# First layer of a four-layer hybrid kernel: tents and masks made in the fourth slot, an image's statistics drawn apart over slots, wide tokens of the last image in half the slots

## The chip, the cores and the metric

The kernel runs on one core of one Trainium2 chip. The metric is the device time of one execution in microseconds; the time given for a kernel is the median of several runs. Beside the times there is one profiled execution, with a record of every instruction on the five engines: PE (TensorE matmul, with PEld for its weight loads), DVE (VectorE), ACT (ScalarE), POOL (GpSimd) and SP (SyncE, which here issues transfers).

## The reference

The input `x` is 4 images of 128 channels by 64 x 64 pixels, float32. Four layers follow each other; the change is in layer 0 alone, so only that one is told in full.

```python
# layer 0: x = x + dcn(group_norm(x))
val = xf @ w_value + b_value                      # 128 channels per token
om  = xf @ w_off + b_off                          # per group (8): 9 offsets (x, y), 9 masks
sy, sx = base_y + offset_y, base_x + offset_x     # 3x3 taps, moved by the offsets
acc = sum over 4 corners: gather(val, corner) * bilinear_weight * inside
out = (acc * mask).sum(over 9 taps) @ w_out + b_out
out = batch_norm(out);  return out * sigmoid(out)
# layer 1: 1x1 conv, depthwise conv, two-way Mamba scan, batch norm, gate
# layers 2 and 3: a token attention and a mixture of experts, each with layer norms
```

Layer 0 is a deformable convolution: each token reads nine places around it, each shifted by an offset that is computed from the token itself.

## The kernel before

Layer 0 works without gathers for nearly all tokens. A token whose offsets stay within one pixel reads only from a 5 x 5 neighbourhood, so its output is a sum of 25 shifted copies of the value map, each times a weight per token and group. The weights come from tent functions of the offsets. The few tokens with larger offsets ("wide tokens") are gathered apart, image by image, and added in.

**Rounds and slots.** Each image is cut into 8 quads of 4 row pairs (`TG` = 4), so there are 32 rounds, `r` = 0 to 31, with four warm-up rounds before and one closing round behind. A round has five slots, `k` = 0 to 4. The order of the instructions on each engine is the order in which the loop writes them: the helper class `InOrder` passes each operation on with a request to keep it in program order, and for that reason all records of layer 0 carry line L85, the helper's own, and are told apart by their tiles. An engine thus stands at an instruction until its inputs are there, and everything behind it on that engine stands too.

What one round does, by engine:

- DVE: five products `pr`, one a slot (`multiply(r, k+1)` in slots 0 to 2, and in the last slot `multiply(r+1, 0)`), each 128 x 2560; in slot 0 `flags(a)` of the round before (it reduces the offsets `omw` to `wide`, compares into `fl`, and counts in `cum`), and after it the generator `weights`, which multiplies the tents by the masks (`tent<-tent,masks`), and over slots 0 to 2 makes `Q` and the weights `wt` of round r+1.
- PE: `accumulate(r, k)`, 20 transposing matmuls a slot that sum the products into `acc`; `project(a, k)`, the projection of the quad `a` = r + 8 (an image ahead) to values and offsets; and small matmuls for ranks and wide tokens.
- ACT: in slot 2 the copy `near_w` of `wt` into PSUM, which the next round's products read; `evict(a, k-1)` in slot k, two copies `omw` and `vb` out of PSUM each, the fourth in slot 4; `onehot` (`ohc`, `ohs`); `finish` (`sl`, a Silu) and `aT`; in slot 3 the copy `xr` (`order`); and at the end of slot 4 `tents(...)` and `near(...)`, the tents `tent`, `ab` and the masks `masks` of round r+2 (four instructions of 128 x 576 for the tents and four small ones for the masks).
- POOL: five pieces of the products (`piece<-v,wt`), the addition of finished quads to `X`, and the indirect gathers of the wide tokens.
- SP: all loads of shifted value tiles `v`, the stores and loads of the offsets.

Buffers bound what can run ahead: `pr` and the gathered `px` have two each, `tent`, `masks` and `wt` have one.

**Side work, one step a slot.** Three generators are advanced by one step in each slot: `weights`; `statistics(n)`, which computes the group-norm statistics of image n and folds them into its weights (`bn_stats` over the image, a matmul `pg` to sum over a group, a second `pg2`, the root `rstd` on ACT, a matmul `pb`, then `bs`, `bn`, `wn` on DVE); and `exceptions(n)`, the wide tokens of an image, which starts in the image's second round: two gathers, tents, weights, then seven times a multiplication of `px` on DVE, seven transposes on PE and the next gather. For image 2 the statistics start in round 3, for image 3 in round 11. All eight `bn_stats` are written in one slot.

**Finishing.** A quad can be finished (`onehot`, then `spread`, `finish`, `settle` in the following slots) when its image's wide tokens are done; the table `ends` says in which round. `flags` and `evict` run for rounds 0 to 23 only, because the last image has nothing ahead of it.

**The end.** `reached` computes from `wide` and `cum` whether any token had larger offsets than the method covers (`m`, `pst`, `pm`, `mm`, `over`); it is written in slot 1 of round 31. The generator `maps_steps`, small work on DVE and PE that prepares matrices for later layers (`omw`, `plm`, `vb`, `xr` as scratch), starts in round 32, two steps a slot. Layer 1 starts behind it.

Of the kernel before, what the change touches and what calls it, by code (L numbers as in the profile page):

```python
# [8 lines left out]
F32 = mybir.dt.float32  # L9
# [8 lines left out]
P = 128  # L18
NB = 4
# [75 lines left out]
class Kernel:  # L95
# [33 lines left out]
    def layer0(self):  # L129
# [8 lines left out]
        R, R2 = 1, 2  # L138
# [11 lines left out]
        with ExitStack() as outer:  # L150
            fp = outer.enter_context(tc.tile_pool(name="d0x", bufs=1))
            over = fp.tile([1, 1], I32, name="over")
            with ExitStack() as ctx:
# [115 lines left out]
                def statistics(n, nc):  # L269

                    xn = X[:, n * L:(n + 1) * L]
                    st = sm.tile([P, 8, 6], F32, name="st", bufs=1)
                    for c in range(8):
                        nc.vector.bn_stats(st[:, c, :], xn[:, c * 512:(c + 1) * 512])
                    mv = sm.tile([P, 2], F32, name="mv", bufs=1)
                    nc.vector.bn_aggr(mv, st)
                    yield
                    pg = pp.tile([P, 512], F32, name="pg", tag="pp")
                    nc.tensor.matmul(pg[:, 0:2], gm, mv, start=True, stop=True)
                    gmv2 = sm.tile([P, 2], F32, name="gmv2", bufs=1)  # L280
                    nc.vector.tensor_copy(gmv2, pg[:, 0:2])
                    d = sm.tile([P, 1], F32, name="d", bufs=1)
                    nc.vector.tensor_sub(d, mv[:, 0:1], gmv2[:, 0:1])
                    nc.vector.tensor_mul(d, d, d)
                    yield
                    pg2 = pp.tile([P, 512], F32, name="pg2", tag="pp")
                    nc.tensor.matmul(pg2[:, 0:1], gm, d, start=True, stop=True)
                    rstd = sm.tile([P, 1], F32, name="rstd", bufs=1)
                    nc.vector.tensor_add(rstd, gmv2[:, 1:2], pg2[:, 0:1])
                    nc.scalar.activation(rstd, rstd, AF.Sqrt, bias=self.eps5)  # L290
                    yield
                    nc.vector.reciprocal(rstd, rstd)
                    ms = sm.tile([P, P], F32, name="ms", bufs=1)
                    nc.vector.tensor_scalar(ms, self.ones, gmv2[:, 0:1], rstd, ALU.mult, ALU.mult)
                    yield
                    pb = pp.tile([P, 512], F32, name="pb", tag="pp")
                    nc.tensor.matmul(pb[:, 0:NWO], ms, w, start=True, stop=True)


                    bs = wp.tile([P, 2, NWO], F32, name="bs", tag="t0")  # L300
                    nc.vector.tensor_sub(bs[:, 0], brow, pb[:, 0:NWO])
                    nc.vector.tensor_copy(bs[:, 1].bitcast(F32R), bs[:, 0])
                    nc.vector.tensor_sub(bs[:, 0], bs[:, 0], bs[:, 1])
                    nc.vector.tensor_scalar(bs[:, 1], bs[:, 1], self.ident[:, 0:1], None, ALU.mult)
                    bn = cp.tile([P, NWO], F32R, name="bn", bufs=2)
                    nc.vector.scalar_tensor_tensor(bn, bs[:, 0], self.ident[:, 1:2], bs[:, 1], ALU.mult, ALU.add)
                    wn = cp.tile([P, NWO], F32, name="wn", bufs=2)
                    nc.vector.tensor_scalar(wn, w, rstd, None, ALU.mult)
                    maps[n] = (wn, bn)
# [336 lines left out]
                ends = {}  # L646
                for i in range(NB * NQS):
                    n, q = divmod(i, NQS)
                    k = 5 + q if n < NB - 1 else (5, 5, 6, 6, 7, 7, 7, 8)[q]
                    ends.setdefault(n * NQS + k, []).append(i)  # L650
                extra, stat, tent, wgen, mask = None, None, None, None, None
                held = marked = None
# [2 lines left out]
                for r in range(-4, LAST_R + 1):  # L655
# [6 lines left out]
                        extra = exceptions(r // NQS)  # L662
                    if r == -3:
                        stat = statistics(1, nc)
                    if r >= 0 and r % NQS == 3 and r // NQS + 2 < NB:
                        stat = statistics(r // NQS + 2, nc)
                    live = 0 <= r < LAST_R
                    coming = 0 <= r + 1 < LAST_R
# [12 lines left out]
                        later_maps = self.maps_begin(left_over)  # L681
                    if 1 <= r <= LAST_R:
                        turn(r - 1)
                    if r == LAST_R:
                        later_maps = self.maps_steps(
                            nc, later_maps, lambda: pp.tile([P, 512], F32, name="plm", tag="pp"))

                    for k in range(W):
                        if live:
                            for u in PIECES.get(k, ()):  # L690
                                accumulate_piece(r)
                            if k < W - 1:
                                accumulate(r, k)
                            if k < W - 2:
                                multiply(r, k + 1)
                        if k == 0 and r > 0:
                            for a in before if before and before[0] >= NQS else ():
                                flags(a)
                        if coming and k < 3:
                            next(wgen)  # L700
                            if k == 2:
                                nc.scalar.copy(near_w, wts[r + 1][:, 1:W - 1])
                        if r <= 0 and before:
                            for a in before if k == 0 else ():
                                rank(a)
                            if k in (1, 3):
                                early = onehot(*which(before[k // 2]), "ohc")
                            if k in (2, 4):
                                collect(before[k // 2 - 1], early)
                        if r < 0 and k < TG:  # L710
                            a = ahead[k // 2]
                            if k % 2 == 0 and a not in ordered:
                                order(a)
                            for h in (0, 1):
                                project(a, 2 * (k % 2) + h)
                            for h in (0, 1):
                                evict(a, 2 * (k % 2) + h)
                        for a in ahead if r >= 0 else ():
                            if k:
                                evict(a, k - 1)  # L720
                            if k < TG:
                                if k == 0 and a not in ordered:
                                    order(a)
                                project(a, k)
                        if stat is not None:
                            next(stat, None)
                        if r > 0:
                            if k == 1:
                                for a in before:
                                    rank(a)  # L730
                            if k == 2:
                                ohc = [onehot(*which(a), "ohc") for a in before]
                            if k == W - 1:
                                for a, oh in zip(before, ohc):
                                    collect(a, oh)
                        if r > 0:
                            if held is not None:
                                settle(held[0], finish(*held))
                                held = None
                            if marked is not None:  # L740
                                i, oh = marked
                                held, marked = (i, spread(i, oh)), None
                            if fins:
                                i = fins.pop(0)
                                marked = i, onehot(*divmod(i, NQS), "ohs", 2)
                            if r == LAST_R - 1 and k == W - 2:
                                fins = ends.pop(LAST_R)
                        if k == TG - 1 and nxt is not None and nxt < NB * NQS:
                            order(nxt)
                        if k == W - 1:  # L750
                            if 0 <= r + 2 < LAST_R and r >= -1:
                                tent, mask = tents(read[r + 2], M, R), near(r + 2)
                            if coming:
                                multiply(r + 1, 0)
                            for a in ahead if r < 0 else ():
                                flags(a)
                        if extra is not None:
                            next(extra, None)
                        if r == LAST_R - 1 and k == 1:
                            reached(nc)  # L760
                        if r == LAST_R:
                            for _ in range(2):
                                next(later_maps, None)
                    before = ahead
# [2068 lines left out]
```

## Time and the profile before

| | |
|---|---|
| time, median of 3 runs | 4961.55 us (4955.89 to 4970.51) |
| the profiled execution's own time | 4962.14 us |
| its span | 4960.0 us |
| mean granted TensorE clock | 0.947 |
| layer 0 in the span | 0 to 860 us; layer 1's first work at 865.5 |
| a steady round (round 8) | 284.14 to 305.42, 21.28 us |
| round 3, round 11 (statistics of images 2 and 3) | 38.85 us, 40.03 us |
| rounds 26 to 28 together | 63.75 us |
| busy in the span | PE 4500.3 us, DVE 3590.7, ACT 3614.6, POOL 3039.9 |

A round is counted from the start of its first product (`pr<-v,wt` on DVE) to the next one. The busy times are of the whole span, so they say little of layer 0, which is a sixth of it. A record has the start in us, the length in us, engine, line, operation, the tile written and the tiles read, the shape and how many alike; in brackets stands how long the engine was idle before it and what released it.

### The profile page before, as it was taken

The page shows a single profiled execution, that of the slowest core. Times are in us where ns is not written, and L with a number is a line of the kernel's source. Part 1 is how long each engine was busy: PE and PEld are TensorE (multiplying, and loading weights), DVE is VectorE, ACT ScalarE, POOL GpSimd, SP SyncE. Part 2 cuts the span into 40 slices and gives each one's busy share as a digit, 9 for nine tenths or more (in the row PEclk, how much of TensorE's full clock was granted, in tenths as well). Part 3 has the DMA queues.
Part 4 walks back from the last instruction along what each step waited for, and adds up shares of the span by engine and source line. Part 5 has one row for each costly group of instructions (what it writes and reads, how often), then busy time and mean ns, then how long its engine had stood idle before and what let it go on. Part 6 is the DMA issues. An engine that isn't in the chain of part 4 may idle for free. (4 is left out here: it accounts for less than half of the span.)

```text
span 4960.0 us, 66029 instructions
## 1 busy us (share of the span) xinstructions
PE 4500.3 (91%) x22570; PEld 2441.0 (49%) x22570; DVE 3590.7 (72%) x7202; ACT 3614.6 (73%) x5503; POOL 3039.9 (61%) x3047
## 2 busy tenths in 40 slices
PE   6788887798899699998897999999999999999798
PEld 4677765465566344443343444444444444444344
DVE  5998996689877578884775666666666666665675
ACT  4455553455555577776675999999999999999575
POOL 1232333155556345553587888888888888878488
PEclk9999999879779799999899999999999999999899
DMA  6666773000000300000000000000000000000000
GB/s 210 165 181 164 184 190 102 5 1 18 11 7 18 96 12 0 1 1 1 18 18 34 1 1 1 1 1 1 1 1 1 1 1 1 1 1 1 7 28 35
DMA packets 65940, 188.39 MB, mean 38 GB/s; under 512 B 12020, under 2 KB 15284, under 8 KB 63924
## 3 DMA queue, kind: packets, MB, share of 16 engines
q1 hardware_dynamic: 60020, 167.89, 12.0%
q0 software_dynamic: 2240, 12.85, 0.9%
q8 instruction: 182, 2.98, 0.3%
q10 hardware_dynamic: 3328, 3.28, 0.2%
q14 instruction: 170, 1.39, 0.1%
HBM read 133.23 MB, written 50.74 MB: 37 GB/s over the span
## 5 line engine op out<-in xcount | busy, mean ns | idle before, releaser
L85 POOL TENSOR_TENSOR r<-r 128x512 f32<-128x512 f32 (+1 forms) x1088 | 1349.2, 1242 | 331.5 <-DVE r L85 267.9
L85 DVE TENSOR_TENSOR r<-r,num 128x1024 f32<-128x1024 f32 (+1 forms) x1088 | 975.2, 927 | 599.6 <-PE num L85 507.5
L85 PE MATMUL D<-F,G 32*128 32x512 f32 (+3 forms) x4608 | 1138.8, 573 | 1.8 <-DVE den L85 0.9
L85 PE MATMUL num<-F,G 32*128 32x512 f32 (+3 forms) x4608 | 1057.2, 590 | 6.8 <-DVE r L85 3.9
L85 ACT ACTIVATE r<-r 128x2048 f32<-128x2048 f32 (+4 forms) x610 | 1018.5, 1679 | 50.9 <-POOL r L85 4.3
L85 ACT ACTIVATE r<-D 128x1536 f32<-128x1536 f32 (+1 forms) x544 | 763.3, 1403 | 50.2 <-PE D L85 29.8
L85 PEld LDWEIGHTS D<-F,G 32*128 32x128 f32 x4608 | 484.5, 184 | 372.9 <-issue 233.7
L85 PE MATMUL acc<-r,v 128*128 128x512 f32 (+3 forms) x1152 | 598.1, 606 | 0.7 <-ACT r L85 0.7
L85 POOL TENSOR_TENSOR x<-x 128x512 f32<-128x512 f32 (+2 forms) x320 | 405.4, 1267 | 146.7 <-DVE m L85 65.0
L85 PEld LDWEIGHTS num<-F,G 32*128 32x128 f32 x4608 | 383.4, 183 | 222.4 <-issue 110.8
L85 PE MATMUL pff<-hid,w_ffn_w2T 128*128 128x512 f32 x1024 | 469.4, 601 | 0.0
L85 PE MATMUL pex<-w_expert_w,vT 128*128 128x512 f32 x1024 | 460.8, 598 | 1.6 <-DVE x L85 1.4
L85 POOL TENSOR_TENSOR piece<-v,wt 128x512 f32<-128x512 f32 x160 | 167.6, 1066 | 380.3 <-DVE cum L85 90.5
L85 PEld LDWEIGHTS acc<-r,v 128*128 128x128 f32 x1152 | 174.1, 188 | 382.7 <-issue 186.7
L85 PE MATMUL acc<-ident,pr 128*128 128x128 f32 x2560 | 320.7, 283 | 42.3 <-DVE pr L85 42.3
L85 ACT ACTIVATE x<-pex,gate 128x128 f32<-128x128 f32 x896 | 256.7, 367 | 101.2 <-PE pex L85 75.7
L85 PEld LDWEIGHTS acc<-ident,pr 128*128 128x128 f32 x2560 | 299.4, 146 | 54.2 <-DVE pr L85 51.7
L85 ACT ACTIVATE hid<-phh,cols 128x512 f32<-128x512 f32 x416 | 252.8, 688 | 68.2 <-PE phh L85 68.0
L85 PEld LDWEIGHTS pex<-w_expert_w,vT 128*128 128x128 f32 x1024 | 190.6, 192 | 216.6 <-issue 160.6
L85 PEld LDWEIGHTS pff<-hid,w_ffn_w2T 128*128 128x128 f32 x1024 | 185.3, 191 | 201.6 <-issue 201.6
L85 DVE TENSOR_TENSOR pr<-v,near_w 128x2560 f32<-128x2560 f32 x96 | 269.9, 2812 | 0.1
L85 POOL TENSOR_TENSOR Y<-y,tm 128x64 f32<-128x64 f32 x256 | 113.3, 463 | 232.2 <-DVE y L85 125.7
(482 smaller groups left out, 7906.6 us busy)
## 6 DMA issues: line engine op xcount, KB each, us to landing
v<-tab SPq DMA_DIRECT2D x320, 256.0 KB
oms<-omw SPq DMA_DIRECT2D x32, 432.0 KB
omr<-oms SPq DMA_DIRECT2D x32, 432.0 KB
X<-in_x_dram SPq DMA_DIRECT2D x8, 1024.0 KB
tab<-vb SPq DMA_DIRECT2D x64, 128.0 KB
o<-o SPq DMA_DIRECT2D x32, 256.0 KB
oin<-o SPq DMA_DIRECT2D x32, 256.0 KB
kept<-X SPq DMA_DIRECT2D x4, 2048.0 KB
```

The lines of the kernel that those rows point to most:

```text
L85: self.last = op(*args, **kwargs)
```

## The change

It has four edits, all in the order of layer 0's instructions; no arithmetic is added or taken away.

1. Tents and masks of round r+2 are written in slot 3 (`W - 2`), ahead of that slot's `evict`, and not at the end of slot 4. In the rounds with r % 8 = 1 in which wide tokens are on, they are written in slot 4, but ahead of its `evict`.
2. The statistics of images 2 and 3 start a round earlier (r % 8 = 2), with two `bn_stats` a slot, and with one more slot after each of the three small matmuls.
3. From round 26 on, the wide tokens go forward by two steps a slot. The last image's quads are finished a round or so earlier (the table `ends`).
4. `reached` moves from slot 1 of round 31 to slot 3, and `maps_steps` starts there, two steps a slot.

```diff
 # statistics(n)
                     for c in range(8):
                         nc.vector.bn_stats(st[:, c, :], xn[:, c * 512:(c + 1) * 512])
+                        if n > 1 and c % 2:
+                            yield
...
                     nc.tensor.matmul(pg[:, 0:2], gm, mv, start=True, stop=True)
+                    if n > 1:
+                        yield
...
                     nc.tensor.matmul(pg2[:, 0:1], gm, d, start=True, stop=True)
+                    if n > 1:
+                        yield
...
                     nc.tensor.matmul(pb[:, 0:NWO], ms, w, start=True, stop=True)
+                    if n > 1:
+                        yield
...
 # the loop over rounds
-                    k = 5 + q if n < NB - 1 else (5, 5, 6, 6, 7, 7, 7, 8)[q]
+                    k = 5 + q if n < NB - 1 else (4, 4, 5, 5, 6, 6, 7, 8)[q]
...
-                    if r >= 0 and r % NQS == 3 and r // NQS + 2 < NB:
+                    if r >= 0 and r % NQS == 2 and r // NQS + 2 < NB:
                         stat = statistics(r // NQS + 2, nc)
...
-                    if r == LAST_R:
-                        later_maps = self.maps_steps(
-                            nc, later_maps, lambda: pp.tile([P, 512], F32, name="plm", tag="pp"))
...
+                        if k == (W - 2 if extra is None or r % NQS != 1 else W - 1) and 0 <= r + 2 < LAST_R and r >= -1:
+                            tent, mask = tents(read[r + 2], M, R), near(r + 2)
                         for a in ahead if r >= 0 else ():
                             if k:
                                 evict(a, k - 1)
...
                         if k == W - 1:
-                            if 0 <= r + 2 < LAST_R and r >= -1:
-                                tent, mask = tents(read[r + 2], M, R), near(r + 2)
                             if coming:
                                 multiply(r + 1, 0)
...
-                        if extra is not None:
-                            next(extra, None)
-                        if r == LAST_R - 1 and k == 1:
+                        for _ in range(1 if r < LAST_R - NQS + 2 else 2):
+                            if extra is not None:
+                                next(extra, None)
+                        if r == LAST_R - 1 and k == W - 2:
                             reached(nc)
-                        if r == LAST_R:
+                            later_maps = self.maps_steps(
+                                nc, later_maps, lambda: pp.tile([P, 512], F32, name="plm", tag="pp"))
+                        if r == LAST_R - 1 and k >= W - 2 or r == LAST_R:
                             for _ in range(2):
                                 next(later_maps, None)
```

## The prediction

> **What bounds the kernel now.** I read the busy table by windows of the first layer first (the change touches nothing behind it: on every engine the instruction order after layer 0 is the same). Layer 0 ends at 860 of the 4960.0 us.
>
> ```profile
> core 0: us, PE busy (x) PEld busy (x) DVE busy (x) ACT busy (x) POOL busy (x), PEclk, DMA share, GB/s
> 240.00:290.00 50.00, 44.69 (x303) 37.98 (x302) 45.37 (x41) 33.23 (x90) 15.18 (x15) 0.97 0.67 175
> ```
>
> DVE is busy 45.4 of 50 us and ACT 33.2. PE shows 44.7, but its own waits are for DVE's products. So a microsecond of DVE idle time is a microsecond of the layer, and the next view is what DVE waits for between 110 and 870 us (total, times, longest).
>
> ```profile
> DVE tent L85 <- ACT masks L85: 26.1, 18, 3.0
> DVE omw L85 <- POOL omw L85: 11.9, 1, 11.9
> DVE bs L85 <- PE pb L85: 11.1, 2, 5.6
> DVE rstd L85 <- PE pg L85: 3.4, 2, 1.8
> DVE m L85 <- PE pst L85: 3.2, 1, 3.2
> DVE rstd L85 <- ACT rstd L85: 1.3, 2, 0.9
> DVE wide L85 <- ACT omw L85: 0.5, 1, 0.5
> ```
>
> These are what the change aims at: the masks, the statistics (`bs`, `rstd`) and the end of the layer (`omw`, `m`). The last line is the one to keep in mind: once, `flags` had to wait for `evict`. Third view, one undisturbed round (8) on ACT, then on DVE:
>
> ```profile
> 284.05 0.56 ACT L85 COPY near_w<-wt 128x480 f32<-128x480 f32 x1 [1.88 <-DVE wt L85]
> 288.43 0.35 ACT L85 COPY omw<-psp 128x216 f32<-128x216 f32 x1
> 288.94 0.81 ACT L85 ACTIVATE tent<-omr,shift 128x576 f32<-128x576 f32 x1
> 291.79 1.08 ACT L85 ACTIVATE masks<-omr,fine 128x72 f32<-128x72 f32 x4
> 292.77 0.57 ACT L85 COPY aT<-acc 128x512 f32<-128x512 f32 x1
> ```
>
> ```profile
> 289.62 0.75 DVE L85 TENSOR_REDUCE wide<-omw 128x4 f32<-128x576 f32 x1
> 290.40 0.66 DVE L85 TENSOR_SCALAR fl<-wide 128x4 f32<-128x4 f32 x1
> 292.90 1.06 DVE L85 TENSOR_TENSOR tent<-tent,masks 128x864 f32<-128x864 f32 x1 [1.39 <-ACT masks L85]
> ```
>
> From `near_w` at 284.05 to the masks' end at 292.87 ACT never pauses; it is a chain of 8.8 us that starts when DVE ends `wt`. DVE has only two products (2.8 us each) and `flags` to put beside it, and idles 1.39 us. `wide` reads the fourth `evict` copy (288.43 to 288.79), and had 0.83 us to spare.
>
> **Part 1, tents and masks ahead of `evict(a, 2)`.** Nothing is added or removed; on ACT tents and masks (292.77 − 288.94 = 3.83 us) go ahead of the last two `evict`s, so these move back by 3.83. The fourth copy ends at 288.79 + 3.83 = 292.62. In DVE's order `flags` stands before the multiplication by the masks, and still reads that copy: the queue behind it is that multiplication, then `Q`, then the next product. `wide` starts at 292.65 instead of 289.62, takes 0.75, and with `fl` and two `cum` 1.31 us (so measured at 143.44 to 144.75, where POOL ran no piece). The masks' multiplication starts at 293.96, where before it started at 292.90: +1.06 us a round. The wait on masks goes, but one on `evict` that is longer takes its place. If `fl` still ran 0.66 us (it ran while POOL multiplied two pieces, 288.94 to 291.03), it would be +1.6.
>
> It holds in the rounds that have an `evict` and no other slack: 1, 5 to 9, 13 to 17, 21 to 24, 15 rounds, +16. Rounds 2, 4, 10, 12, 18 have 6 to 8 us between copy and `wide`, and pay nothing; 3 and 11 lie behind the statistics; from 25 on nothing is evicted and the masks' wait (mostly under 0.5 there) goes for nothing. In round 13 the chain takes in one more table load for Silu (1.28 us at 384.34, which stood in round 11), in rounds 19 and 20 some 0.6 us. Sum +17.7; bounds +13 (`flags` finds slack in a few rounds) and +26 (`fl` stays slow).
>
> The Trainium skill, SBUF — State Buffer, Terms, calls the read and write port pair of DVE and GpSimd an exclusive lock held for a whole instruction; the 0.66 us of `fl` beside a POOL piece (0.17 elsewhere) agrees, and as the pieces would then run in DVE's idle time the rule speaks for 1.06.
>
> **Part 2, statistics.** The same eight `bn_stats`, spread over four slots of rounds 2 and 10, and four more slots between the short steps. Before, in round 3:
>
> ```profile
> 187.50 0.16 DVE L85 TENSOR_TENSOR rstd<-gmv,pg 128x1 f32<-128x1 f32 x1 [1.76 <-PE pg L85]
> 188.02 0.16 DVE L85 RECIPROCAL rstd<-rstd 128x1 f32<-128x1 f32 x1 [0.36 <-ACT rstd L85]
> 195.21 0.51 DVE L85 TENSOR_TENSOR bs<-brow,pb 128x344 f32<-128x344 f32 x1 [5.64 <-PE pb L85]
> ```
>
> The two rounds idle 15.8 us in these waits. The `pb` wait goes, as `bs` comes a slot later. But the square root is now in ACT's queue behind `near_w` (0.5), an `evict`, the tents (3.83) and another `evict`, and the reciprocal, in the last slot, waits: counted from the end of `wt` at 185.74, the next `pr` started 12.18 later before; now the reciprocal at about +7.4, the `pr` at +7.9, and 2.7 us of `bs`, `bn`, `wn` still to come in round 4. Gain 1.55. In round 11 the same with `sl` 0.67 and the table load 1.28 ahead of the root: 12.49 before, 12.58 after, loss 0.1. Sum −1.5; bounds −15.8 (every wait hidden) and +3 (one more table change of 1.28 a time).
>
> **Part 3, wide tokens of the last image, two steps a slot from round 26.** Seven multiplications of 1.08 us, 49 transposes and five gathers, the same number; only closer together.
>
> ```profile
> px<-tab,idx POOLq DMA_INDIRECT x28, 6.8
> ```
>
> A gather lands 6.8 us after its issue (median; single ones 4.4 to 11.2). There are two `px` buffers, so tile s+2 needs the multiplication of s (1.1), its transposes behind PE's queue (about 2.5) and the gather: 10.4 us. Two slots last 8.5 us (rounds 26 to 28 took 63.75 us, 15 slots). So DVE stalls some 2 us at every second one of the five later tiles, three times: +6. Until now a tile had four slots, 17 us. Bounds +0.5 (landing in 4.4) and +10 (landing in 11.2, with the products queued behind on DVE).
>
> The Trainium skill, DMA: Bandwidth & Descriptors, "Anatomy of one DMA — SWDGE (gpsimd) path", gives 2.0 us plus bytes over 436e3: by it a gather of 459 KB takes an estimated 3.05 us, nothing would stall, and the sum below would be some 6 us less; the trace's 6.8 is what I use.
>
> **Part 4, the end.** The images' last `finish` steps come one round earlier (three in round 28). PE then stands behind `oT`, which ACT copies after the tents: some 1.5 us in round 29 and 0.2 in 30, while masks' waits of about 1.5 go: +0.2, bounds −1 and +4. At the end of the layer:
>
> ```profile
> 829.52 0.22 DVE L85 COPY omw<-ident 128x128 f32<-128x128 f32 x1
> 841.67 0.40 DVE L85 TENSOR_SCALAR omw<-omw 128x1 int32<-128x1 int32 x5 [11.94 <-POOL omw L85]
> ```
>
> The small chain of layer 1's maps starts at 841.67 and ends at 859.94; it takes 18.3 us, and layer 1 starts behind it. Without `reached` (822.05 to 826.84) ahead of it the last product ends 4 us sooner, about 824.9; the last sum on PE ends at 832.8, `reached` at 834.5, and the chain starts at about 834.8, its steps two a slot from round 31. −6.9; bounds −4 (the chain meets the last sums on PE) and −11 (its small matmuls, which ran at half clock: granted 0.64 in 850 to 870, weight loads 0.34 us where others take 0.19, run at full).
>
> **Sum.** 17.7 − 1.5 + 6 + 0.2 − 6.9 = +15.5. The profiled execution took 4962.14 us (0.6 above the median of three, 4961.55, which ran from 4955.89 to 4970.51); the forecast is 4961.55 + 15.5 = 4977. No change that a measurement can tell is ±0.3%, 4946.7 to 4976.4, so the forecast sits on its upper edge.
>
> **Rivals.**
> 1. Faster: `flags` doesn't gate. Place: DVE's `wide` in slot 0. Price: then the 26.1 us on masks go whole, −26.1 − 1.5 + 6 + 0.2 − 6.9 = −28, 4933. It decides at the fourth copy's end: up to 289.62 in round 8's time `wide` waits for nothing. For: the masks' wait is real, 18 times. Against: the copy is put at 292.62 by adding ACT's own rows, with no pause among them to absorb it, and round 6 shows the wait already (0.5). Chance 0.08.
> 2. No difference: `flags` costs its 13 to 17, but the statistics' waits go by half (−8), gathers land early (+1) and the end gains 9: 0, with a range of ±8, about 4962. For: 15.8 us of visible waits, and half clock at the end. Against: ACT's queue ahead of the root. 0.20.
> 3. Much slower: the `fl` collision stays (+8.5), and the gathers land late (+10 instead of +6) with PE's in-order queue behind the transposes (+4): 4992 to 5000. For: gathers of 11.2 us are in the trace. Against: they are few. 0.17.
>
> My own case has 0.55, 4967 to 4987, half of it above the bound: 0.29 slower and 0.26 the same. With rival 2 wholly within (0.17; 0.01 faster, 0.02 slower) and rival 3 slower: slower 0.48, same 0.43, faster 0.09. Range: from 4954, which takes in most of rival 2, to 4995, which takes in the low end of rival 3.
>
> **What would show it.** Right: DVE's `wide` waiting for ACT's `omw` some 15 times, about 3 us each; the masks' wait near zero; a steady round of 22.35 us where it was 21.28; `rstd` waiting for ACT's `rstd` twice, several us; `px` waiting for its gather in rounds 26 and 27; the maps' chain starting about 7 us sooner against the last product. Wrong: a steady round shorter than 21.28 (rival 1); statistics rounds of 3 and 11 shorter by 5 us or more (rival 2); DVE idle by over 4 us at one `px` (rival 3).

## The result, and the profile after

The changed kernel takes 4989.04 us (median of 8 runs, 4983.89 to 4996.12); the kernel before, run beside it, 4961.09 us (8 runs). The ratio is 1.0058, 95% interval 1.0045 to 1.0071: slower by 28 us (22 to 35). The forecast was 4977, slower by 15.5; 4989 lies inside the forecast's range (4954 to 4995) and just above the 4967 to 4987 of its own case.

First the waits of DVE in the changed kernel, from 110 us to the end of layer 0 (total, times, longest):

```profile
DVE wide L85 <- ACT omw L85: 47.4, 17, 4.6
DVE rstd L85 <- ACT rstd L85: 13.5, 2, 9.0
DVE pr L85 <- PE acc L85: 9.9, 8, 2.6
DVE px L85 <- DMA px<-tab,idx: 6.8, 2, 5.7
DVE m L85 <- PE pst L85: 4.9, 1, 4.9
DVE tent L85 <- ACT masks L85: 3.2, 2, 1.8
```

The three largest waits that the change aimed at are gone or small: masks 26.1 to 3.2, `bs` on `pb` 11.1 to nothing, `omw` on POOL 11.9 to nothing. (`rstd` still waits for `pg`, 3.5 us, and `m` waits longer than before.) In the place of each stands a new one. Round 8 on ACT shows the first:

```profile
287.74 0.56 ACT L85 COPY near_w<-wt 128x480 f32<-128x480 f32 x1 [1.88 <-DVE wt L85]
291.23 0.76 ACT L85 ACTIVATE tent<-omr,shift 128x576 f32<-128x576 f32 x1
294.04 1.08 ACT L85 ACTIVATE masks<-omr,fine 128x72 f32<-128x72 f32 x4
295.92 0.34 ACT L85 COPY omw<-psp 128x216 f32<-128x216 f32 x1
```

and the same round on DVE:

```profile
296.29 0.75 DVE L85 TENSOR_REDUCE wide<-omw 128x4 f32<-128x576 f32 x1 [2.89 <-ACT omw L85]
297.07 0.17 DVE L85 TENSOR_SCALAR fl<-wide 128x4 f32<-128x4 f32 x1
297.61 1.05 DVE L85 TENSOR_TENSOR tent<-tent,masks 128x864 f32<-128x864 f32 x1
```

The masks are done at 295.1, but the multiplication that reads them starts at 297.61: `flags` stands ahead of it in DVE's order and waits 2.89 us for the fourth `evict`, which is now the last of ACT's chain. `fl` takes 0.17 us, not 0.66. The round lasts 22.29 us, 1.01 more than before.

By stages of layer 0, from the rounds' starts in the two profiled executions (us):

| stage | before | after | difference | forecast |
|---|---|---|---|---|
| rounds 0, 1, 5 to 9, 13 to 25 | 458.5 | 474.9 | +16.4 | +17.7 |
| rounds 2 to 4 (statistics) | 81.9 | 80.5 | -1.4 | -1.55 |
| rounds 10 to 12 (statistics) | 83.1 | 86.1 | +3.0 | +0.1 |
| rounds 26 to 28 (wide tokens) | 63.8 | 76.7 | +12.9 | +6 |
| rounds 29 and 30 | 39.4 | 44.2 | +4.8 | +0.2 |
| round 31 to layer 1 | 51.6 | 44.7 | -6.9 | -6.9 |
| together | 778.3 | 807.1 | +28.8 | +15.5 |

Layer 1 is counted here from its first instruction on POOL (at 865.48 us in the kernel before). In runs below that change nothing in rounds 2 to 4 and 10 to 12, these two stages take 80.4 to 81.9 and 83.1 to 85.6 us, so up to 1.5 and 2.5 us of their differences can be variation between executions.

### The profile page after: what moved, and what is told of

It reads as the page before. It is cut to its first block, busy times and chain, and to the rows that moved or that the text cites. A ratio compares the mean times of both kernels' runs of the same rounds, so it can differ in the third digit from the quotient of the medians.

```text
span 4986.8 us, 66012 instructions
## 1 busy us (share of the span) xinstructions
PE 4504.9 (90%) x22570; PEld 2445.7 (49%) x22570; DVE 3589.0 (72%) x7202; ACT 3616.0 (73%) x5503; POOL 3041.8 (61%) x3047
```

## The experiments

Each time is given against the kernel before, run beside it on the same chip (there its median was 4954 to 4956 us). Stage times are from one profiled execution each. Some stretches vary between executions of the same instructions: the warm-up ahead of round 0 by up to 4 us, the two statistics stages by up to 2.5, round 31 to layer 1 by up to 6 (47.8 to 53.8 us where nothing was changed there), and all that stands behind layer 0 by up to 24 (4077 to 4101 us). So stages are compared from round to round, and whole times by the ratios alone.

**1. Each edit by itself.** Four kernels, the kernel before with one of the four edits of the diff above.

> Only edit 1: tents and masks ahead of the fourth slot's evict; all else as before. Theory (flags wait for the evict that now stands behind the tents): DVE's wide waits for ACT's omw some 3 us in each of the 15 rounds with an evict and without slack, a steady round is 22.3 us, and the statistics rounds 3 and 11, in which pb waits for a PSUM buffer that an evict frees, become up to 3.8 us longer each. Together +18 to +26 us. Rival (the moved statistics bring most of the wait on wide with them, the tents alone cost little): +10 or less, a steady round of 21.3 us or shorter.

Measured 1.0032 (1.0020 to 1.0043), +16 us. From round 0 to the start of round 31 it lost 17.85 us; a steady round lasts 22.30 us, and `wide` waits 49.2 us in 19 places. Of the 17.85, 15.2 lie in the rounds of the table's first line. The theory holds, the rival falls. Of the extra loss in the statistics rounds there is less than I allowed: +0.4 in round 3, +2.4 in round 11, where either round varies by up to 1.5 between executions.

> Only edit 2: statistics a round earlier and spread over slots; tents stay at the end of slot 4. Theory (the root stood in ACT's queue behind the tents, which cost 3.83 us in round 3 and as much in round 11): without the tents ahead of it rounds 2 to 4 together are 5 us shorter than before and rounds 10 to 12 about 1 us shorter; -6 us in all. Rival (the wait for the root is made by the other work ahead of it in the queue, Silu's wait for PE and a table load): about +1.6 us as in the whole change, -1.4 and +3.0.

Measured 0.9990 (0.9978 to 1.0003), which doesn't tell it from no change. The root is reached earlier without the tents, as the theory says: its wait is 0.71 us in round 3 and 5.27 in round 11, where the changed kernel has 4.49 and 9.05. But the rounds do not get shorter by that: rounds 2 to 4 gain 2.0 us, rounds 10 to 13 lose 1.8, and most of both can be variation between executions. Part of it came back at once, in round 4:

```profile
196.40 2.60 DVE L85 TENSOR_TENSOR_SCAN cum<-ones,cum,fl 128x4 f32<-128x4 f32 x1
196.90 2.07 POOL L85 TENSOR_TENSOR piece<-v,wt 128x512 f32<-128x512 f32 x2
```

The first line is DVE's, the second POOL's. `cum` is 0.23 us elsewhere; here it ends with POOL's two pieces, which themselves stood behind a gather. So the theory named the queue rightly, and its -6 us are not there.

> Only edit 3: the last image's wide tokens two steps a slot from round 26, and its quads finished a round earlier. Theory (gathers that land too late for the two px buffers, and POOL pieces that start late behind a gather and then hold up DVE): rounds 26 to 28 some 13 us longer than before and rounds 29 and 30 some 5 us longer, as in the whole change; +17 us. Rival (rounds 29 and 30 lost because tents stand ahead of the finishing in ACT's queue): +13 us and rounds 29 and 30 as before.

Measured 1.0026 (1.0012 to 1.0041), +13 us. Rounds 26 to 28 are 14.8 us longer, rounds 29 and 30 5.5. The rival falls: tents stand in slot 4 here, and rounds 29 and 30 lose as much. What I had not expected is behind them: round 31 to layer 1 is 13.5 us shorter, without the fourth edit.

> Only edit 4: reached and the maps' small chain from slot 3 of round 31. Theory: the last product ends 4 us earlier and the chain starts behind the last sum instead of after the closing round's other work; layer 1 starts 7 us earlier, -7 us. Rival (the layer's end is set by the sums and the finishing of the last quads, not by the chain): within 2 us of before.

Measured 1.0004 (0.9994 to 1.0014): no gain. The maps' chain does start sooner, 24.2 us after the start of round 31 where the kernel before and the run with the statistics alone have 27.8. But it then takes 18.7 us, where those two have 17.9 and 15.1. The end of the layer is 3.3 us shorter in its profile, but 3.8 in that of the statistics alone, where nothing at the end was changed, so no gain at the end can be put down to the edit. The theory's 7 us are refuted; by the interval the edit alone gains at most 3.

**2. Is it flags?**

```diff
-                        if k == 0 and r > 0:
-                            for a in before if before and before[0] >= NQS else ():
-                                flags(a)
                         if coming and k < 3:
                             next(wgen)
                             if k == 2:
                                 nc.scalar.copy(near_w, wts[r + 1][:, 1:W - 1])
+                        if k == 0 and r > 0:
+                            for a in before if before and before[0] >= NQS else ():
+                                flags(a)
```

> The changed kernel with flags(a) written behind the first step of weights (masks and Q) instead of ahead of it. Theory (the changed kernel's rounds are held by flags, which wait for the evict behind the tents, with the masks' multiplication queued behind them): the wait of wide on omw falls from 2.9 us to under 0.5, the multiplication waits for the masks instead, which end at about 7.4 us after near_w, some 1.9 us; a steady round of about 21.1 us, 1.2 us less than the changed kernel, -17 us against it, that is +8 to +12 us against the kernel before. Rival (evict itself is late for other users, PE's PSUM buffers or the store of the offsets): steady round stays at 22.3 us.

Measured 1.0037 (1.0023 to 1.0050), +18 us where the changed kernel has +28. Round 8 on DVE:

```profile
290.95 1.06 DVE L85 TENSOR_TENSOR tent<-tent,masks 128x864 f32<-128x864 f32 x1 [1.75 <-ACT masks L85]
293.69 0.75 DVE L85 TENSOR_REDUCE wide<-omw 128x4 f32<-128x576 f32 x1
```

`wide` waits for nothing, the multiplication for the masks, 1.75 us; the round is 21.20 us (expected 21.1). For the round that is the theory, nearly to its numbers; `flags` was what held it. The gain on the changed kernel is less than the theory's 17 us: some 10 by the two ratios, 11.7 by the profiles from round 0 to the start of round 26. The run also says why the place in slot 3 could never bring much: from `near_w` to the masks' end ACT still needs 7.4 us, and DVE has two products, 5.6 us, to put beside it. In the kernel before, `flags` filled that gap.

**3. Another place for the tents.** Two kernels, the kernel before with one edit each: tents and masks in slot 1 behind the second step of `weights`, and at the head of slot 2 (in both, rounds with r % 8 = 1 keep them in slot 4, since the wide tokens use the same buffers then). The code below is the second's; its comment says how the first differs.

```diff
+                        if k == 2 and 0 <= r < LAST_R - 2 and r % NQS != 1:    # or: k == 1, behind next(wgen)
+                            tent, mask = tents(read[r + 2], M, R), near(r + 2)
                         if coming and k < 3:
                             next(wgen)
```

> The kernel before with one edit: tents and masks written in slot 1, behind the second step of weights, where ACT is idle for 6 us of a round (in rounds with r % 8 = 1 at the end of slot 4 as before). Theory (what matters is the length of ACT's chain from near_w to whatever DVE needs first; the tents fit into ACT's idle time before near_w): the wait on masks goes without a new one on omw, a steady round of 19.9 to 20.3 us, -18 to -26 us. Rival (near_w becomes late behind the tents, and all products with it): a steady round of 21.3 us or more, no gain.

Measured 1.0170 (1.0156 to 1.0185), +84 us: far from the theory's -18 to -26, and for another reason than the rival's. DVE in round 15, then the sum of that wait over the layer:

```profile
522.11 0.22 DVE L85 SCALAR_TENSOR_TENSOR slot<-cum,rk,fl 128x4 f32<-128x4 f32 x1 [3.91 <-ACT rk L85]
```

```profile
DVE slot L85 <- ACT rk L85: 75.0, 21, 4.0
```

`rank` is written later in slot 1 than the tents, so its small copy `rk` on ACT now stood behind 3.9 us of tents, and DVE's `slot`, with a product behind it, waited for it in 21 rounds. I had looked for what reads the tents and not for what else stands behind them.

> As the kernel with the tents in slot 1, but written at the head of slot 2, so that in ACT's order they stand behind the rank copy rk and not ahead of it. Theory (what the tents stand ahead of decides: in slot 1 they stood ahead of rk, for which DVE's slot waited 3.9 us a round; here they stand ahead of only the two wt copies, in ACT's idle time): no wait on rk, none on masks, none on omw; a steady round of 19.8 to 20.1 us against 21.28; -22 to -28 us. Rival (near_w or the first product becomes late behind tents and the wt copies): a wait of pr on wt of 1 us or more, a steady round of 21 us or more.

Measured 0.9949 (0.9929 to 0.9968), -25 us: faster than both kernels. Round 8, ACT and then DVE:

```profile
293.40 0.78 ACT L85 ACTIVATE tent<-omr,shift 128x576 f32<-128x576 f32 x1 [2.58 <-DVE t L85]
296.22 1.08 ACT L85 ACTIVATE masks<-omr,fine 128x72 f32<-128x72 f32 x4
297.77 0.56 ACT L85 COPY near_w<-wt 128x480 f32<-128x480 f32 x1
```

```profile
293.77 0.21 DVE L85 SCALAR_TENSOR_TENSOR slot<-cum,rk,fl 128x4 f32<-128x4 f32 x1
297.78 2.83 DVE L85 TENSOR_TENSOR pr<-v,wt 128x2560 f32<-128x2560 f32 x1 [0.19 <-ACT wt L85]
```

The tents start as soon as DVE has read the old ones (`t`), run while ACT would have idled, and end in time for `near_w`; the next product starts after DVE's usual 0.19 us. A steady round lasts 19.88 us with 0.43 us of DVE idle in it.

**4. The wide tokens and the ends apart.**

> The kernel before with only the two steps a slot from round 26; the table of ends as before. Theory (gathers): rounds 26 to 28 together 13 to 15 us longer, rounds 29 and 30 and the end of the layer as before; +14 us. Rival (the third finishing in round 28 and the earlier ones in PE's and ACT's queues make a good part of it): +8 us or less in rounds 26 to 28.

Measured 1.0020 (1.0010 to 1.0030), +10 us; rounds 26 to 28 +13.9, rounds 29 and 30 -0.1, the end as before. So the 13 us belong to the two steps and the loss in rounds 29 and 30 to the ends.

> The kernel before with two steps a slot from round 26 and the old table of ends, and the last image's five later gathers left out: tiles 2 to 6 of its wide tokens are multiplied and transposed from the buffers that are there, so the wide tokens of the last image get other values; nothing else is left out. Theory (the 14 us of the two steps are landing times of the gathers and POOL's pieces that start late behind them): rounds 26 to 28 as in the kernel before or shorter, 62 to 65 us, against 76 to 78 with the gathers. Rival (the closer multiplications and transposes themselves hold PE and DVE up): 70 us or more.

Measured 0.9998 (0.9985 to 1.0012). Rounds 26 to 28 last 64.0 us, against 63.8 before and 77.6 with the gathers. The steps themselves cost nothing; the gathers, with what they do to POOL's queue, cost it all. How, the changed kernel's rounds 26 and 27 show; DVE first, then POOL:

```profile
742.78 3.47 DVE L85 TENSOR_TENSOR t<-tent 128x864 f32<-128x864 f32 x1
755.80 1.09 DVE L85 TENSOR_TENSOR px<-px,wt 128x896 f32<-128x896 f32 x1 [1.09 <-DMA px<-tab,idx]
766.42 1.09 DVE L85 TENSOR_TENSOR px<-px,wt 128x896 f32<-128x896 f32 x1 [5.71 <-DMA px<-tab,idx]
```

```profile
742.23 0.99 POOL L85 DMA_INDIRECT px<-tab,idx  x1 [6.34 <-PE pe L85]
743.24 2.07 POOL L85 TENSOR_TENSOR piece<-v,wt 128x512 f32<-128x512 f32 x2
758.18 3.40 POOL L85 DMA_INDIRECT px<-tab,idx  x1
```

Two `px` wait for their gathers, 6.8 us. The longer wait is not landing alone: PE's transposes had freed the buffer at 755.91, but POOL stood at the addition of a finished quad, so the gather began at 758.18, and it took 3.40 us to issue where most take 0.95 to 0.99. The lines ahead of it, DVE's product and POOL's addition:

```profile
756.81 3.91 DVE L85 TENSOR_TENSOR pr<-v,wt 128x2560 f32<-128x2560 f32 x1
756.04 1.99 POOL L85 TENSOR_TENSOR X<-X,sl 128x512 f32<-128x512 f32 x1 [3.33 <-ACT sl L85]
```

The rest is the second mechanism: a gather waits at the head of POOL's queue for PE's transposes, and the product's pieces behind it start late, beside DVE's `t` (1.05 us elsewhere), which ends 0.94 us after them. Besides, two products wait 2.1 us together for PE's sums, and `wt` 0.7 for a piece.

> The kernel before with only the table of ends changed, and so that one step a slot is enough: (5, 5, 5, 6, 6, 6, 7, 8). Three quads are finished in each of rounds 29 and 30, one in 31. Theory (the last 13 us of the two-step kernel's end came from the quads finished earlier, since the maps' chain waits for POOL behind the additions of the last quads): from round 31 to layer 1 10 to 13 us shorter, rounds 29 and 30 up to 5 us longer; -5 to -12 us in layer 0. Rival (the end's length is set by the PE clock, not by the finishing): no gain at the end, +3 to +5 us.

Measured 0.9996 (0.9987 to 1.0005), no difference that can be told. By stages both halves of the theory are there: round 31 to layer 1 10.6 us shorter, as the maps' chain starts 4.7 us sooner after the round's start (it waits 4.27 us for POOL and not 11.94) and itself takes 12.8 us (14.9 to 17.9 in the profiles with the old ends and `reached` in its old place); rounds 29 and 30 3.8 us longer, where a third finish is worked into a round. In round 30 DVE waits for the masks, made by ACT behind the finishing:

```profile
807.37 1.06 DVE L85 TENSOR_TENSOR tent<-tent,masks 128x864 f32<-128x864 f32 x1 [5.95 <-ACT masks L85]
```

**5. Together.** Tents at the head of slot 2, ends as in the last kernel, one step of the wide tokens a slot, `reached` and maps as before, and the statistics spread as in the change with more empty slots, so that none of DVE's steps waits in slots 3 and 4.

> The kernel with the tents at the head of slot 2, and besides: statistics spread as in the change but with two more empty slots behind pg2 and behind pb, so that no step of them that waits falls into slots 3 and 4; and the table of ends (5, 5, 5, 6, 6, 6, 7, 8) with one step of the wide tokens a slot. Theory: as the kernel with the tents alone, rounds 2 to 5 and 10 to 13 together another 8 to 14 us shorter (the waits for pg, rstd and pb go), the end of layer 0 another 3 to 7 us; -35 to -45 us against the kernel before. Rival (what the waits lose comes back as collisions of POOL and DVE, as in the statistics alone): -25 to -30 us.

Measured 0.9957 (0.9941 to 0.9973), -21 us: no better than the tents alone, less than the theory and even than the rival. The waits for `pg`, the root and `pb` are all gone, but four of DVE's products stand, 4.0 and 4.2 us in rounds 4 and 5, 4.9 and 6.3 in rounds 12 and 13, each until 0.1 us after PE's sum of an earlier product has ended (the profile names the sum as releaser for the last alone). That one on DVE, and what stood on PE before it:

```profile
418.75 2.82 DVE L85 TENSOR_TENSOR pr<-v,near_w 128x2560 f32<-128x2560 f32 x1 [6.28 <-PE acc L85]
```

```profile
410.59 1.51 PE L85 MATMUL pb<-w,ms 128*128 128x344 f32 x2 [5.59 <-ACT vb L85]
```

`pb` was written in slot 2, and its PSUM buffer comes free by an `evict` that stands behind `near_w`; PE stood there 5.59 us, with the next products' sums behind it. Ahead of the other three it stood 5.2 to 6.2 us in the same way, at `pg2` twice and at `pb`.

The last run moves the empty slots. The code is that of `pg2`; `pb` has the same. `pg2` and `pb` are then written in slot 4 and read in slot 0:

```diff
+                    for _ in range(2 if n > 1 else 0):
+                        yield
                     pg2 = pp.tile([P, 512], F32, name="pg2", tag="pp")
                     nc.tensor.matmul(pg2[:, 0:1], gm, d, start=True, stop=True)
-                    for _ in range(3 if n > 1 else 0):
+                    if n > 1:
                         yield
```

> As the kernel with all (tents at the head of slot 2, statistics spread, ends (5, 5, 5, 6, 6, 6, 7, 8)), with one edit: the two empty slots of the statistics stand ahead of the matmuls pg2 and pb, not behind them, so that their PSUM buffers are read in the next slot instead of three slots later. Theory (in the kernel with all, pg2 and pb each held one of the two PSUM buffers that project and evict share, for three slots; PE stood at the next projection, and DVE's products waited for PE's sums, 4.0 and 4.2 us in rounds 4 and 5, 4.9 and 6.3 in 12 and 13): these waits go, rounds 2 to 6 and 10 to 14 together 10 to 18 us shorter than there; -35 to -45 us against the kernel before. Rival (the waits of PE come from the extra small matmuls and the products' order, not from the buffers): rounds 4, 5, 12 and 13 as in the kernel with all, -20 to -25 us.

Measured 0.9913 (0.9895 to 0.9932), 4908.57 us, -43 us: the best of all kernels here, faster than the kernel before by 34 to 52 us. Rounds 4, 5, 12 and 13 have no wait of 1 us or more on DVE, and from round 0 to the start of round 31 it is 32.4 us shorter than the kernel before. The expectation's size holds; its reason only in part, as the lines above have PE at `pb` and `pg2` themselves and not at a projection behind them: what mattered was where they stood in PE's queue against the `evict` that frees their buffer. Here PE stands 1.13 and 1.80 us at the two `pg2` and not at all at `pb`.

## Why the prediction was right, and where it was not

The direction, the range and the first step were right. Tents and masks ahead of `evict`: +1.06 us a round was worked out, 1.01 measured; the rounds that the step counted lost 16.4 us in the changed kernel and 15.2 with that edit alone, for 17.7, and moving `flags` took the wait away. The rival without a gate is refuted by the same run. `fl` did fall to 0.17 us, so the lower of the two prices held. The statistics of image 2 were sized rightly too: in round 3 the next product starts 7.86 us after the end of `wt`, for 7.9.

Four terms of the sum were not.

**Wide tokens, +6 for +12.9.** The step reckoned three stalls of some 2 us from landing times alone. DVE waited for gathers in two places, 6.8 us, and the longer of the two came mostly from a gather that POOL began and issued late. What the step left out is POOL's order: a gather stands behind an addition, and one that waits for PE holds the pieces behind it, and these then meet DVE's work. DVE's busy time in rounds 26 to 28 rose by 3.3 us, with the same seven multiplications of `px` in them. The prediction's bound of +10 was too low for the same reason. Rival 3 had this stage nearly right (+10 for late gathers, +4 for PE's queue), and its sign, DVE idle by over 4 us at one `px`, came; its other term, the slow `fl`, did not.

The Trainium skill, DMA: Bandwidth & Descriptors, "Anatomy of one DMA — SWDGE (gpsimd) path", gives the fit of 2.0 us plus bytes over 436e3, an estimated 3.05 us for such a gather. The five gathers of these rounds landed 4.8 to 8.1 us after their issue began (median of all 28: 6.4, and 6.8 before), so for these indirect gathers the measurement decides against it.

The Trainium skill, SBUF — State Buffer, Terms, says that the loser of the port pair that DVE and GpSimd share is blocked for the other's whole instruction. `cum` at 2.60 us, ending 0.03 us after POOL's pieces, and `t` at 3.47, ending 0.94 us after them (its own length is 1.05), agree with it; so do they with any lock of that kind, which no run here takes apart.

**Statistics of image 3, +0.1 for +3.0.** The stage's +3.0 can be variation in good part, but counted as the step counts it the loss is there: the next product starts 12.43 us after the end of `wt`, where the step had 9.9. The root's wait was put at what stood ahead of it in ACT's queue; of that queue I had the busy times, but not that one of them would wait itself:

```profile
394.43 0.78 ACT L85 ACTIVATE sl<-pO,bbi,bsc 128x512 f32<-128x512 f32 x1 [2.38 <-PE pO L85]
399.38 1.28 ACT L85 ACT_TABLE_LOAD   x1
400.68 0.29 ACT L85 ACTIVATE rstd<-rstd,eps 128x1 f32<-128x1 f32 x1
```

The Silu `sl` waited 2.38 us for PE, which had itself stood 5.21 us at `pg2` until an `evict` freed its PSUM buffer; all behind `sl` moved, and the reciprocal on DVE stood 9.05 us. Rival 2's sign, rounds 3 and 11 shorter by 5 us or more, came (9.5 and 5.0) and tells nothing: rounds 2 and 10, into which their work had moved, are 5.2 and 5.1 us longer.

**Earlier finishing, +0.2 for +4.8.** I costed PE's wait for one copy. A third finish in a round lengthens ACT's and PE's queues in the round after: the changed kernel has it in round 28, and round 29 is 6.0 us longer, round 30 1.2 shorter. In round 29 DVE's product waits 2.61 us for PE, which waited 3.79 for ACT's `sl`, and with the tents in slot 4 the masks come 5.95 us late.

**The end, -6.9 for -6.9, is luck.** I put it down to `reached` and the maps' early start. The step that the last product ends 4 us sooner once `reached` is out of its way failed: it ends 15.5 us after the start of round 31, where it was 15.8, since DVE now waits there for PE's sums (1.05, 1.02 and 2.15 us). Alone, the edit gave nothing that can be told, while the new ends alone shortened the end by 10.6 to 13.5 us. With both, the changed kernel has less than that: `reached`, moved behind the last product, waits 4.93 us for PE's sums ahead of `pst`, where it waited 3.15 (7.53 with the edit alone), and the maps' chain takes 17.1 us, where it took 12.8 with the third edit alone. The likeliest reading is that the fourth edit took some of the ends' gain back; as the end varies by up to 6 us between profiles, it isn't shown.

The three misses of size add up to 14.4 us; the first step gave 1.3 of them back, and the forecast fell short by the remaining 13.

## What to carry to other kernels

When a step is moved forward in an engine's queue, list what now stands behind it and who waits for each of these; the step's own reader is only one of them. A move into the engine's idle time, here between one buffer's last read and the next chain's first instruction, gains what a move inside the busy chain can't. The same holds for a shared buffer or a transfer: put a matmul where its buffer is already free, and a gather where nothing urgent stands behind it in its queue.

## What the runs showed of the hardware

An indirect gather's issue took POOL 0.95 to 0.99 us mostly. In three traces (the changed kernel, the third edit alone, the two steps alone) one took 3.40 us, each time in the same setting. A product of two operands in SBUF, begun on DVE during an addition on POOL, took 3.9 us instead of 2.82 and ended 2.7 us after the addition; the gather's issue, begun during the product, ended 0.9 us after it. So each took about its usual time once the one ahead had ended. Products that read `near_w` from PSUM kept 2.81 us beside two POOL pieces. Tiny DVE operations (0.17 to 0.23 us) took 2.6 to 2.77 us beside a gather's issue and the two pieces behind it. And what stands behind layer 0 differed by up to 24 us between executions of the same instructions, so that a change of a few microseconds in layer 0 could be read from stages only.
